# A Mamba block and a binarised feed-forward on one core: one transfer over 128 partitions for xc, z and the gated outputs, norm's affine kept off DVE, other durations in the planner

## The chip, the cores and the metric

The kernel runs on one core of one Trainium2 chip. The metric is the device time in microseconds of one execution, as a median over runs. A profiled execution, taken by the hardware profiler, stands beside it. The engines are called PE (matrix multiply), DVE (vector), ACT (scalar, activations), POOL (GpSimd) and SP (the engine that issues almost every DMA here).

## The reference, cut to what matters

The input x holds B = 8 images of C = 384 channels and L = 1024 positions, in float32. Two residual steps follow each other.

```
x = x + conv_ref(ln_c(x), ...)            # a Mamba block with an MLP
t = to_tokens(x)
x = from_tokens(t + ffn_ref(ln_t(t), ...))   # binarised weights, quantised activations

conv_ref:  t = layernorm(t) * ln_w + ln_b
           xm, z = split(t @ in_proj_w.T)              # 768 + 768 channels
           xc = silu(depthwise conv of 3 taps over positions of xm)
           dt, Bm, Cm = split(xc @ x_proj_w.T)         # 24, 16, 16
           dt = softplus(dt @ dt_proj_w.T + dt_proj_b)
           h[l] = exp(dt[l] * A) * h[l-1] + dt[l]*xc[l] * Bm[l]      # 768 x 16 states
           y = (h * Cm summed over 16) + xc * D
           t = (y * silu(z)) @ out_proj_w.T
           t = gelu(t @ mlp_w1.T + b1) @ mlp_w2.T + b2
ffn_ref:   y = t @ sign(W1 - mean).T + b1, quantised per image; gelu; the same with W2
```

The feed-forward changes images 0 to 4 only: 8 images in 5 groups of one image, and the rest stays zero.

## The kernel before

**Stages of an image.** `s1(b)` normalises the image (`norm`), applies ln_w and ln_b (`affine`, one per 128 channels), multiplies with in_proj_w, makes xc, dt and dt*xc, and z in `gate`. It works in two halves of T = 512 positions and writes xc, z, dt and dtx to DRAM. `s2(b)` is the scan. `s3(b)` reads the gated outputs yg, multiplies with out_proj_w and runs the MLP. `ffn(b)` is the second residual step. `binarise` makes the signs of W1 and W2 once, beside image 0.

**The scan.** One scan tile holds 32 channels x 4 states on 128 partitions. ACT makes `da` = exp(dt*A), POOL makes `u` = dtx*B, DVE runs the recurrence (line 888), and DVE or POOL multiplies by C (lines 905 and 902). PE adds up the states with the matrix `fold` into the PSUM tile `py` (line 838). A *unit* is one `py`: an ACT instruction puts xc*D into it, from the tile `xr`; at its end DVE multiplies by `zr`, in place, and `zr` is stored as `yg_d` (lines 855 and 861). Images 1 to 6 are scanned over the full width (`half` is None): a unit is then 64 channels x both halves, and an image has 12 units, each with two tiles per quarter of the states. Images 0 and 7 are scanned in two halves, with 128 channels x 512 positions per unit, six units per half. Image 7 keeps its gated outputs in SBUF. The rings for `xr` and `zr` have one buffer each, those for the weights `w_b` and `w_f` three.

**The layout in DRAM.** xc, z and yg are handed over as [NP, P, T]: 12 pairs of 32-channel groups, and within a pair first the 64 channels of half 0, then those of half 1. A full-width unit is one contiguous block of 128 rows of 2 KB. In `s1` and `s3`, where 128 channels of one half lie on the partitions, the same data is moved by two transfers of 64 partitions each, one for even pairs and one for odd ones (`by_pair`, line 597, and line 928). So are the units of images 0 and 7 (line 801).

**The order of the work.** Each operation is written down with an engine, an assumed duration, and the tiles it reads and writes. `Plan.run` then simulates the five engines with these durations and emits the instructions in the order in which its simulation starts them; each engine executes its own list strictly in order. `MM`, `SWITCH` (added to a group of `py` matmuls), `SIGNAL` (one engine's wait for another) and the figures of the DMA line set its clock:

```
            if e == "SP":
                dma_free = max(dma_free, end + 1.0) + op.size / 370e3
                end = dma_free + 0.9
```

Where the simulated PE would idle for over 0.7 us, it emits spare matmuls that nothing reads. `affine` is an operation of ACT by default that DVE may take (and POOL, where `pool` is set, as for the norm) when ACT is busy in the simulation. So other durations mean another order on every engine.

Of the kernel before, what the change touches and what calls it, by code (L numbers as in the profile page):

```python
# [26 lines left out]
F32 = mybir.dt.float32  # L27
# [6 lines left out]
P = 128  # L34
# [34 lines left out]


MM = 0.86
SWITCH = 0.34
BATCH = 2
SIGNAL = 0.1
IDLE = 0.7
EARLY = 2
FRONTS = 3
# [84 lines left out]
class Plan:  # L162
# [57 lines left out]
    def run(self):  # L220
# [60 lines left out]
        while left:  # L281
            best = None
            for e in self.ENGINES:
                able = [(s, op) for op in cands[e] if (s := start_of(op)) is not None]
                first = max(free[e], min(able, key=lambda a: a[0])[0]) if able else None
                if first is not None and (best is None or first < best[0]):
                    best = first, e, able, False
                for op in guests[e]:
                    s = start_of(op)
                    if s is None:  # L290
                        continue
                    s = max(free[e], s)
                    if s + HOST < free[op.engine] and (
                        first is None or s + op.others[e][0] <= first
                    ) and (best is None or s < best[0]):
                        best = s, e, [(s, op)], True
            now, e, able, guest = best
            op = able[0][1] if guest else choose(e, now, able)
            if guest:
                op.cost, op.emit = op.others[e]  # L300
            for k in op.others:
                guests[k].remove(op)
            cands[op.engine].remove(op)
            op.engine = e
            if op.settle is not None:
                op.settle(ahead("POOL", now) - ahead("DVE", now), drop)
            if op.prio[0] == 0:
                scanned = max(scanned, op.prio[1])
            left -= 1
            if e == "PE":  # L310
                while now - free[e] > IDLE and self.spare.ring.free[0:] and (
                    self.spare.ring.free[0] + SIGNAL <= free[e]
                ):

                    ring = self.spare.ring
                    heapq.heappop(ring.free)
                    self.spare.real = ring.make(self.spare.shape, self.spare.name)
                    self.fill()
                    free[e] = clock.run(free[e], MM / 2)
                    heapq.heappush(ring.free, free[e])  # L320
            for t in taken_by(op):
                heapq.heappop(t.ring.free)
                t.ring.taken[t.lane] += 1
                t.real = t.ring.make(t.shape, t.name)
            op.emit()
            cost = op.cost
            if op.table is not None and op.table != table:
                cost += LOAD_TABLE
                table = op.table
            end = free[e] = clock.run(now, cost) if e == "PE" else now + cost  # L330
            if e == "SP":
                dma_free = max(dma_free, end + 1.0) + op.size / 370e3
                end = dma_free + 0.9
            for t in op.tiles:
                if t.ring is not None:
                    t.left -= 1
                    t.last = max(t.last, end)
                    if not t.left:
                        heapq.heappush(t.ring.free, t.last)
            for n in op.next:  # L340
                n.wants -= 1
                n.ready = max(n.ready, end + n.slack + (
                    0.0 if n.engine == e != "SP" and not n.others else SIGNAL
                ))
                if not n.wants:
                    cands[n.engine].append(n)
                    for k in n.others:
                        guests[k].append(n)


class Layer:
    def __init__(self, ctx, tc, a, out):
# [38 lines left out]
        for b in range(B):  # L391
            for name in ("dt", "dtx"):
                self.dram[name, b] = handed(f"{name}_d{b}", [DI, L])

            for name in ("xc", "z", "yg"):
                self.dram[name, b] = handed(f"{name}_d{b}", [NP, P, T])
            self.dram["rows", b] = handed(f"rows_d{b}", [2 * NS, L])
            if b < NQ:
                self.dram["mid", b] = handed(f"mid_d{b}", [C, L])
                self.dram["y1", b] = handed(f"y1_d{b}", [P, KH, L])  # L400
# [6 lines left out]
        self.nc.tensor.matmul(  # L407
            first, self.ones, self.one.to_broadcast([P, T]), start=True, stop=True
        )
        self.plan.spare = self.piece("mm", [P, T], "spare")  # L410
        self.plan.fill = lambda: self.nc.tensor.matmul(
            self.plan.spare.real[:, : 2 * P], self.ones,
            self.one.to_broadcast([P, 2 * P]), start=True, stop=True,
        )

    def piece(self, ring, shape, name):
# [90 lines left out]
    def affine(self, out, in_, r, w, bias=0.0, scale=1.0, n=T, pool=False):  # L507
# [16 lines left out]

            return emit

        others = {"DVE": (c_dve(n), on(nc.vector))}
        if pool:
            others["POOL"] = (0.18 + n * 0.00095, on(nc.gpsimd))
        extra = 0.0 if plain else 0.06 if isinstance(scale, float) else 0.13  # L530
        self.plan.add("ACT", 0.16 + n * 0.00083 + extra, on_act, r=r, w=w, others=others)

    def norm(self, t, eps, scale):
# [17 lines left out]
        def spread(src, name):  # L551
            p = self.piece("mm", [P, T], name)

            def emit():
                for g in range(G):
                    one = self.ident[:, g * DQ : g * DQ + 1].to_broadcast([P, P])
                    nc.tensor.matmul(
                        p.real[:, g * TG : (g + 1) * TG], one, src.real, start=True, stop=True
                    )

            add("PE", 1.25, emit, r=[src], w=[p])
            return p

        p_sum = columns(t, "p_sum")
# [23 lines left out]
    def s1(self, b):  # L588
# [5 lines left out]

        def by_pair(name, half, t):
            d = self.dram[name, b]
            for i in range(2):
                to = d.real[i::2, half * DP : (half + 1) * DP, :].rearrange("k p l -> p k l")
                self.store(
                    to, t, lambda x, i=i: x[i * DP : (i + 1) * DP, :, :], [d[half, i]],  # L600
                    4 * DP * KD * T, 0.6,
                )

        def tiled(name, half, t):
            d = self.dram[name, b]
# [29 lines left out]
        for half, cols in enumerate(HALVES):  # L635
# [51 lines left out]
                            start=(k == 0), stop=(k == KC - 1),  # L687
                        )

            add("PE", 0.2 + KC * MM, low, r=[w, *all_m], w=[p_dbc], claim=[dbc])  # L690
            self.affine(lambda dbc=dbc: dbc.real, lambda p_dbc=p_dbc: p_dbc.real, [p_dbc], [dbc])
            p_bc = self.piece("mm", [P, TG], "p_bc")
            rows = self.piece("rstd", [P, TG], "rows")
# [61 lines left out]
    def scan(self, b, half, state):  # L755
# [30 lines left out]
        for m in range(DI // per_unit):  # L786
            py = self.piece("y", [P, T], "py")
            tiles = [range((2 * m + i) * wide, (2 * m + i + 1) * wide) for i in both]

            def rows_of(m=m):  # L790

                if half is None:
                    return [(slice(0, P), m, slice(0, P))]
                mine = slice(half * DP, (half + 1) * DP)
                return [(slice(i * DP, (i + 1) * DP), 2 * m + i, mine) for i in both]

            def unit(name):
                r = self.piece(f"{name[0]}r", [P, T], f"{name[0]}r")
                d = self.dram[name, b]
                keys = [(h, i) for h in halves for i in both]  # L800
                for at, pair, its in rows_of():
                    self.plan.add("SP", 0.35, lambda at=at, pair=pair, its=its: (
                        nc.sync.dma_start(r.real[at, :], d.real[pair, its, :])
                    ), r=[d[k] for k in keys], w=[r], size=4 * P * n // wide)
                return r

            skip = self.d_pair if half is None else self.d_unit
# [48 lines left out]
                zr.real, py.real, zr.real  # L856
            ), r=[py], w=[zr])
            d = self.dram["yg", b]
            for at, pair, its in rows_of():
                self.plan.add("SP", 0.35, lambda at=at, pair=pair, its=its, zr=zr: (  # L860
                    nc.sync.dma_start(d.real[pair, its, :], zr.real[at, :])
                ), r=[zr], w=[d[h, pair] for h in halves], size=4 * P * n // wide)

    def on_pool(self, i, q, m):

# [44 lines left out]
    def s3(self, b):  # L910
        nc, a, add = self.nc, self.a, self.plan.add
        yg_d = self.dram["yg", b]
        for half, cols in enumerate(HALVES):
# [11 lines left out]
                    late.append((w, pm))  # L925
            else:
                yg = self.piece("yg", [P, KD, T], "yg")
                for i in range(2):
                    src = yg_d.real[i::2, half * DP : (half + 1) * DP, :]
                    self.plan.add("SP", 0.6, lambda i=i, yg=yg, src=src: nc.sync.dma_start(  # L930
                        yg.real[i * DP : (i + 1) * DP, :, :], src.rearrange("k p l -> p k l")
                    ), r=[yg_d[half, m] for m in range(i, NP, 2)], w=[yg[i]],
                        size=4 * DP * KD * T)
            for m in range(KC):
                if b == B - 1:
                    w, pm = late[m]
# [1 line left out]
                else:  # L938
                    w = self.weights("w6", KD, a["out_proj_w"][m])
                    pm = self.piece("mm", [P, T], "p_out")  # L940
                    self.matmuls(pm, w, yg, 0, KD, True, True, [yg[0], yg[1]], [t2])
                self.affine(
                    lambda m=m, t2=t2: t2.real[:, m, :], lambda pm=pm: pm.real, [pm], [t2[m]]
                )
# [320 lines left out]
```

## Time and profile before

| | us |
|---|---|
| median of 3 runs | 3303.43 (3297.44 to 3304.55) |
| profiled execution | 3289.89 |
| its span, first to last instruction | 3287.1 |
| stage 0 to 345, mostly images 0 and 1 before their gated outputs | 345 |
| stage 345 to 2836, the units of images 1 to 6 | 2491 |
| stage 2836 to the end, image 7 | 451 |

In the page, "busy" is the time in which an engine had an instruction running. An engine can be busy while its instruction is held up, which a mean far above the shortest time of the same group shows. In a table by stretches the last columns are the granted PE clock, the mean busy share of the 16 DMA engines and the rate in GB/s. In the DMA issues the last figure is the median time from issue to landing. The chain of waits is followed back from the last instruction; "issue" in it is time for which the profile shows no cause.

### The profile page before, as it was taken

To read this page: it belongs to the slowest core of one execution; us is meant where nothing else is said; L and a number is where in the kernel's file an instruction comes from. 1 tells how busy PE (TensorE), PEld (TensorE's weight loads), DVE (VectorE), ACT (ScalarE), POOL (GpSimd) and SP (SyncE) were. 2 spreads that over 40 slices of the span, in tenths; PEclk is the share of its full clock that TensorE was granted. 3 is DMA by queue.
4 is the path that set the end of the run, shared out by engine and by line. 5 is a ranking of instruction groups with operands and counts; after the bars stand their busy time and mean duration, and the time that the engine had idled before them with its cause. 6 is when DMAs were issued, how large, how long until landed. Compare 5 with 4: busy or idle time off the path is not lost.

```text
span 3287.1 us, 34264 instructions
## 1 busy us (share of the span) xinstructions
PE 3136.3 (95%) x11184; PEld 1327.2 (40%) x11184; DVE 2769.7 (84%) x2139; ACT 2023.0 (62%) x2241; POOL 2848.0 (87%) x1369
## 2 busy tenths in 40 slices
PE   8988889999989999899998999999999999999999
PEld 4333434344333444334443443444433444344444
DVE  4679799899897899888898888799996998887980
ACT  4778577667655566655674665676556555565651
POOL 1688789988899989899989999989999999999970
PEclk9999999999999999999999999999999999999999
DMA  6998778857786677876688665976778666666542
GB/s 219 288 284 245 218 230 282 279 181 232 232 293 219 192 220 247 280 225 211 235 259 253 228 204 192 312 242 210 228 235 292 211 193 211 217 205 220 177 133 77
DMA packets 368083, 748.74 MB, mean 228 GB/s; under 512 B 34593, under 2 KB 111905, under 8 KB 367905
## 3 DMA queue, kind: packets, MB, share of 16 engines
q1 hardware_dynamic: 367472, 746.46, 71.4%
q8 instruction: 89, 1.46, 0.2%
q14 instruction: 90, 0.73, 0.1%
q10 hardware_dynamic: 432, 0.09, 0.0%
HBM read 566.06 MB, written 180.36 MB: 227 GB/s over the span
## 4 chain that ended last, share of the span: by engine, by line
PE 71%; DMA 8%; ACT 7%; DVE 6%; issue 3%; POOL 3%; SPq 1%; DVEq 0%; POOLq 0%; ACTq 0%
PE p_o L485 15%; PE p_y L485 14%; PE p_h L485 13%; PE py L838 8%; PE p_out L485 7%; PE p_in L485 5%; PE p_z L485 5%; DVE da L888 2%; DMA w_b<-in_mlp_w 2%; ACT da L501 2%; ACT L501 1%; POOL u L884 1%; DVE u L888 1%; DMA w_n<-bin_w 1%; PE p_dt L716 1%
## 5 line engine op out<-in xcount | busy, mean ns | idle before, releaser
L884 POOL TENSOR_TENSOR u<-dtx_r,bc 128x1024 f32<-128x1024 f32 x768 | 1790.1, 2365 | 54.0 <-DMA dtx_r<-dtx_d 32.4
L501 ACT ACTIVATE da<-dt_r,a_neg 128x1024 f32<-128x1024 f32 (+1 forms) x960 | 901.9, 945 | 549.6 <-DVE u L905 340.3
L902 POOL TENSOR_TENSOR u<-u,bc 128x1024 f32<-128x1024 f32 x352 | 829.2, 2367 | 141.0 <-DVE u L888 136.7
L888 DVE TENSOR_TENSOR_SCAN da<-da,u 128x1024 f32<-128x1024 f32 (+1 forms) x416 | 840.4, 2020 | 75.6 <-ACT da L501 40.3
L888 DVE TENSOR_TENSOR_SCAN u<-da,u 128x1024 f32<-128x1024 f32 (+1 forms) x352 | 699.0, 2009 | 84.0 <-ACT da L501 43.6
L485 PE MATMUL p_h<-t,w_b 128*128 128x512 f32 x1152 | 515.0, 601 | 17.2 <-DMA w_b<-in_mlp_w 17.2
L905 DVE TENSOR_TENSOR u<-da,bc 128x1024 f32<-128x1024 f32 x416 | 507.9, 1221 | 10.7
L485 PE MATMUL p_o<-g,w 128*128 128x512 f32 x1152 | 506.4, 595 | 0.0
L838 PE MATMUL py<-u,fold 128*32 128x512 f32 x3072 | 374.9, 602 | 5.5 <-POOL u L902 2.9
L485 PE MATMUL p_y<-gf,w_n 128*128 128x512 f32 x720 | 324.0, 605 | 22.4 <-ACT gf L501 13.4
L485 PEld LDWEIGHTS p_h<-t,w_b 128*128 128x128 f32 x1152 | 216.1, 191 | 303.5 <-issue 277.9
L485 PEld LDWEIGHTS p_o<-g,w 128*128 128x128 f32 x1152 | 216.1, 190 | 287.0 <-issue 281.5
L485 PE MATMUL p_y<-tn,w_b 128*128 128x512 f32 x720 | 324.0, 597 | 1.7 <-DVE tn L582 1.6
L501 ACT ACT_TABLE_LOAD x226 | 290.0, 1283 | 8.6 <-DVE xc L655 3.8
L485 PE MATMUL p_out<-yg,w 128*128 128x512 f32 x552 | 250.7, 606 | 14.5 <-DMA dtx_r<-dtx_d 6.0
L485 PE MATMUL p_in<-t,w_f 128*128 128x512 f32 x504 | 232.3, 608 | 16.5 <-DMA w_f<-in_in_proj_w 10.6
L485 PE MATMUL p_z<-t,w_f 128*128 128x512 f32 x504 | 226.4, 596 | 9.4 <-DMA w_f<-in_in_proj_w 5.7
L485 PEld LDWEIGHTS p_y<-gf,w_n 128*128 128x128 f32 x720 | 136.3, 193 | 208.9 <-issue 175.2
L485 PEld LDWEIGHTS p_y<-tn,w_b 128*128 128x128 f32 x720 | 133.5, 190 | 176.1 <-issue 154.7
L516 ACT ACTIVATE g<-p_h,v_vecs 128x512 f32<-128x512 f32 x156 | 105.8, 682 | 137.8 <-PE p_h L485 137.4
L838 PEld LDWEIGHTS py<-u,fold 128*32 128x32 f32 x3072 | 81.0, 110 | 265.4 <-issue 207.4
L516 ACT ACTIVATE y<-p_y,v_vecs 128x512 f32<-128x512 f32 x138 | 93.9, 682 | 129.5 <-PE p_y L485 86.7
(115 smaller groups left out, 2745.9 us busy)
## 6 DMA issues: line engine op xcount, KB each, us to landing
dtx_r<-dtx_d SPq DMA_DIRECT2D x144, 512.0 KB, 4.9
dt_r<-dt_d SPq DMA_DIRECT2D x144, 512.0 KB, 5.5
w_b<-in_mlp_w SPq DMA_DIRECT2D x192, 192.0 KB, 2.8
w<-in_mlp_w SPq DMA_DIRECT2D x96, 384.0 KB, 3.2
w_f<-in_in_proj_w SPq DMA_DIRECT2D x168, 192.0 KB, 4.2
y_d<-y SPq DMA_DIRECT2D x120, 256.0 KB, 4.2
gf<-y_d SPq DMA_DIRECT2D x20, 1536.0 KB, 9.0
xc_d<-xc SPq DMA_DIRECT2D x32, 768.0 KB, 8.8
```

What stands on the lines that cost most here:

```text
L485: self.nc.tensor.matmul(p.real, w.real[:, w0 + k, :], t.real[:, k0 + k, :], start=start and k == 0, stop=stop and k == n - 1,)
L501: lambda: self.nc.scalar.activation(out(), in_(), func, **{k: v() if callable(v) else v for k, v in kw.items()}),
L516: nc.scalar.activation(out(), in_(), AF.Identity, bias=bias, scale=scale)
L716: add("PE", MM, lambda k=k, pd=pd, dbc=dbc, w=w: nc.tensor.matmul(pd.real, w.real[:, k % KC, :], dbc.real, start=True, stop=True,), r=[dbc ...
L838: nc.tensor.matmul(py.real[p0 : p0 + DQ, :], self.fold, hc, start=False, stop=(q == NQUAD - 1), skip_group_check=True,)
L884: add("POOL", 2.36, lambda: nc.gpsimd.tensor_mul(u.real, dtx_r.real, spread(bq)), r=[dtx_r, bq], w=[u])
L888: add("DVE", (0.2 if half else 0.15) + n * 0.00209, lambda k=k, col=col: nc.vector.tensor_tensor_scan(to.real[:, k, :], da.real[:, k, :], ...
L902: add("POOL", 2.36, lambda: nc.gpsimd.tensor_mul(u.real, u.real, spread(cq)), r=[cq], w=[u])
L905: add("DVE", 1.21, lambda: nc.vector.tensor_mul(u.real, da.real, spread(cq)), r=[da, cq], w=[u])
```

## The change

Five things are edited.

1. xc, z and yg are laid out as [KD, 2, P, T]: six groups of 128 channels, then the half, then the channel within the group. `by_pair`, the yg load in `s3` and the units of images 0 and 7 become one transfer of 128 partitions each. A full-width unit takes 64 of the 128 channels of a group, from both halves.
2. `affine` with `pool` set may go to ACT or POOL, and no longer to DVE.
3. `SWITCH`, `SIGNAL`, the figures of the DMA line, the added durations in `affine`, those of `spread` in `norm` and of `low` in `s1` change, and a `DRAIN` of 0.2 us is added to every wait of another engine for PE.
4. `unread` is called up front: two POOL fills, three POOL products, two matmuls, an ACT copy and a DVE scan, with strided operands, on three buffers of the ring tag `u`; nothing reads their results.
5. The wait of out_proj for yg is on the whole tile.

```diff
-SWITCH = 0.34
+SWITCH = 0.26
-SIGNAL = 0.1
+SIGNAL = 0.05
+DRAIN = 0.2
...
-                dma_free = max(dma_free, end + 1.0) + op.size / 370e3
-                end = dma_free + 0.9
+                dma_free = max(dma_free, end + 0.8) + op.size / 395e3
+                end = dma_free + 0.75
...
-                ))
+                ) + (DRAIN if e == "PE" != n.engine else 0.0))
...
-                self.dram[name, b] = handed(f"{name}_d{b}", [NP, P, T])
+                self.dram[name, b] = handed(f"{name}_d{b}", [KD, 2, P, T])
...
+    def unread(self, sbuf, psum):
+        nc = self.nc
+        w = sbuf.tile([P, L], F32, tag="u", name="w_once", bufs=9)
+        v = sbuf.tile([P, L], F32, tag="u", name="v_once", bufs=9)
+        o = sbuf.tile([P, L], F32, tag="u", name="o_once", bufs=9)
+        pm = psum.tile([P, T], F32, tag="mm", name="p_once", bufs=3)
+        nc.gpsimd.memset(w, 0.5)
+        nc.gpsimd.memset(v, 0.5)
+        for i in (2, 4):
+            n = L // i
+            nc.gpsimd.tensor_mul(
+                o.rearrange("p (n i) -> p n i", i=i), w.rearrange("p (n i) -> p n i", i=i),
+                v[:, :n].unsqueeze(2).to_broadcast([P, n, i]),
+            )
+        nc.gpsimd.tensor_mul(
+            o.rearrange("p (n i) -> p i n", i=2), w.rearrange("p (i n) -> p i n", i=2),
+            v.rearrange("p (i n) -> p i n", i=2),
+        )
+        pairs = w.rearrange("p (n i) -> p n i", i=2)
+        for _ in range(2):
+            nc.tensor.matmul(pm[:DQ, :], self.fold, pairs[:, :, 0], start=True, stop=True)
+        nc.scalar.copy(o.rearrange("p (n i) -> p n i", i=2)[:, :, 0], w[:, :T])
+        nc.vector.tensor_tensor_scan(
+            o.rearrange("p (n i) -> p n i", i=2)[:, :, 1], v[:, :T], pairs[:, :, 1], 0.0,
+            ALU.mult, ALU.add,
+        )
...
-        others = {"DVE": (c_dve(n), on(nc.vector))}
         if pool:
-            others["POOL"] = (0.18 + n * 0.00095, on(nc.gpsimd))
+            others = {"POOL": (0.18 + n * 0.00095, on(nc.gpsimd))}
+        else:
+            others = {"DVE": (c_dve(n), on(nc.vector))}
-        extra = 0.0 if plain else 0.06 if isinstance(scale, float) else 0.13
+        extra = 0.0 if plain else 0.09 if isinstance(scale, float) else 0.18
...
-            for i in range(2):
-                to = d.real[i::2, half * DP : (half + 1) * DP, :].rearrange("k p l -> p k l")
-                self.store(
-                    to, t, lambda x, i=i: x[i * DP : (i + 1) * DP, :, :], [d[half, i]],
-                    4 * DP * KD * T, 0.6,
-                )
+            self.store(d.real[:, half].rearrange("k p l -> p k l"), t, lambda x: x, [d[half]],
+                       4 * P * KD * T)
...
-            def rows_of(m=m):
+            def rows_of(d, m=m):
                 if half is None:
-                    return [(slice(0, P), m, slice(0, P))]
-                mine = slice(half * DP, (half + 1) * DP)
-                return [(slice(i * DP, (i + 1) * DP), 2 * m + i, mine) for i in both]
+                    return d.real[m // 2, :, m % 2 * DP : (m % 2 + 1) * DP, :]
+                return d.real[m, half]
...
-                keys = [(h, i) for h in halves for i in both]
-                for at, pair, its in rows_of():
-                    self.plan.add("SP", 0.35, lambda at=at, pair=pair, its=its: (
-                        nc.sync.dma_start(r.real[at, :], d.real[pair, its, :])
-                    ), r=[d[k] for k in keys], w=[r], size=4 * P * n // wide)
+                keys = list(halves)
+                self.load(r, lambda t: t, rows_of(d), r=[d[k] for k in keys], size=4 * P * T,
+                          cost=0.35)
...
-            for at, pair, its in rows_of():
-                self.plan.add("SP", 0.35, lambda at=at, pair=pair, its=its, zr=zr: (
-                    nc.sync.dma_start(d.real[pair, its, :], zr.real[at, :])
-                ), r=[zr], w=[d[h, pair] for h in halves], size=4 * P * n // wide)
+            self.store(rows_of(d), zr, lambda t: t, [d[h, m] for h in halves], 4 * P * T, 0.35)
...
-                for i in range(2):
-                    src = yg_d.real[i::2, half * DP : (half + 1) * DP, :]
-                    self.plan.add("SP", 0.6, lambda i=i, yg=yg, src=src: nc.sync.dma_start(
-                        yg.real[i * DP : (i + 1) * DP, :, :], src.rearrange("k p l -> p k l")
-                    ), r=[yg_d[half, m] for m in range(i, NP, 2)], w=[yg[i]],
-                        size=4 * DP * KD * T)
+                self.load(yg, lambda t: t, yg_d.real[:, half].rearrange("k p l -> p k l"),
+                          r=[yg_d[half, m] for m in range(KD if b == 0 else NP)], size=4 * P * KD * T)
```

More of the change, by code (lines that the diff above doesn't have):

```diff
@@ L409, in __init__ @@
         )
+        self.unread(sbuf, psum)
         self.plan.spare = self.piece("mm", [P, T], "spare")
@@ L559, in emit @@
                     )
-            add("PE", 1.25, emit, r=[src], w=[p])
+            add("PE", 0.98, emit, r=[src], w=[p])
             return p
@@ L688, in low @@
                         )
-            add("PE", 0.2 + KC * MM, low, r=[w, *all_m], w=[p_dbc], claim=[dbc])
+            add("PE", 0.26 + KC * MM, low, r=[w, *all_m], w=[p_dbc], claim=[dbc])
             self.affine(lambda dbc=dbc: dbc.real, lambda p_dbc=p_dbc: p_dbc.real, [p_dbc], [dbc])
@@ L940, in s3 @@
                     pm = self.piece("mm", [P, T], "p_out")
-                    self.matmuls(pm, w, yg, 0, KD, True, True, [yg[0], yg[1]], [t2])
+                    self.matmuls(pm, w, yg, 0, KD, True, True, [yg], [t2])
                 self.affine(
```

## The prediction, made before the changed kernel ran

> **What bounds the kernel now.** I read the page's busy shares first, then the table by stretches, the DMA issues, the groups of line 523 with the chain of waits, and last the waits of the SP queue.
>
> ```profile
> PE 3136.3 (95%) x11184; PEld 1327.2 (40%) x11184; DVE 2769.7 (84%) x2139; ACT 2023.0 (62%) x2241; POOL 2848.0 (87%) x1369
> ...
> q1 hardware_dynamic: 367472, 746.46, 71.4%
> ```
>
> PE has work for 95% of the span, 100.3 us of it being the planner's spare matmuls. POOL and DVE follow closely. The 16 DMA engines are on average busy 71.4%: less than a third of their time is free.
>
> ```profile
> 345.00:2836.00 2491.00, 2394.93 (x8634) 1003.90 (x8633) 2212.40 (x1598) 1550.69 (x1607) 2292.18 (x1054) 0.99 0.74 234
> 82.00:400.00 318.00, 274.09 (x1025) 121.14 (x1024) 248.47 (x243) 227.06 (x309) 251.43 (x156) 0.94 0.86 264
> 1340.00:1350.00 10.00, 6.28 (x20) 3.25 (x20) 7.61 (x8) 7.35 (x9) 7.21 (x4) 1.00 1.05 405
> ```
>
> Columns after the length: busy PE, weight load, DVE, ACT, POOL, clock, DMA share, GB/s. The first row is the stage in which images 1 to 6 are scanned: 72 units of 34.6 us, DMA share 0.74 at 234 GB/s. The second is the busiest long stretch (0.86). The third is the fastest of all 10 us stretches: 405 GB/s, or 25.3 GB/s per engine. Over the whole run an engine moves 746.46 MB / (0.714 x 16 x 3287.1 us) = 19.9 GB/s while it is busy.
>
> ```profile
> xr<-xc_d SPq DMA_DIRECT2D x72, 256.0 KB, 3.0
> zr<-z_d SPq DMA_DIRECT2D x72, 256.0 KB, 3.2
> yg_d<-zr SPq DMA_DIRECT2D x72, 256.0 KB, 2.2
> yg<-yg_d SPq DMA_DIRECT2D x28, 768.0 KB, 10.4
> dt_d<-dt SPq DMA_DIRECT2D x16, 1536.0 KB, 7.5
> ```
>
> Each unit of that stage loads xr and zr and stores yg_d, once each, and they land in 2.2 to 3.2 us. A yg load of half the partitions takes longer (10.4 us) than a store of twice the bytes over 128 (7.5 us).
>
> ```profile
> L523 DVE TENSOR_SCALAR t<-t,v_vecs 128x512 f32<-128x512 f32 x12 | 29.4, 2468 | 0.1
> ```
>
> The chain of waits at that line:
>
> ```profile
> 932.40 0.26 DVE t L523
> 932.66 9.73 issue
> 942.39 0.02 DVEq L888
> 942.41 4.75 issue
> 947.17 0.54 DVE t L523
> ```
>
> Twelve instructions with a shortest time of 0.519 us average 2.468 us. Two in a row took 15.38 us from 932.32, while POOL ran without a gap, and the chain carries 9.73 + 4.75 = 14.5 us of that. Three more took 8.39 us from 2350.86 (3.4 us in the chain).
>
> ```profile
> SPq L803 <- DMA yg_d<-zr: 51.1, 41, 6.7
> ```
>
> SP issues in order, and the next zr load already waits behind the landing of the yg_d store.
>
> [...]
>
> **The change part by part**, against the profiled execution of 3289.89 us, which lies 13.5 us under the median of 3303.43; differences are added to the median.
>
> The unit transfers. With the layout [KD, 2, P, T] a unit of a full-width scan takes `d.real[m // 2, :, m % 2 * DP : ..., :]`: two blocks of 64 rows, far apart. The instruction lists show the DRAM side as 2 x 64 x 512 where it was 128 x 512, in 72 xr loads, 72 zr loads and 72 yg_d stores. [...] In 345 to 2836 us the kernel moves 234 x 2491 = 583 MB, of it 216 x 0.262 = 56.6 MB in these transfers. Engines 0 and 1 would each carry (583 - 56.6)/16 + 56.6/2 = 32.9 + 28.3 = 61.2 MB, where now it is 36.4. At 25.3 GB/s that is 2419 us of work, at 19.9 GB/s 3075 us, in a stage of 2491 us. I take the fast rate, as the 14 other engines are then lightly loaded, and the fill of the busiest long stretch, 0.86: 2419/0.86 = 2813 us, **+322 us**. Bounds: filled completely at the fast rate it fits (0 from bandwidth alone); 0.86 at the slow rate gives +1085. Queued behind them are all weights, dt_r and dtx_r of SP: PE takes a w_b of 192 KB every 2.58 us (12 records of p_h, two such weights, are 5.15 us in the chain) from three buffers, a cover of 3 x 2.58 - 2.8 (its landing) = 4.9 us, less than one such transfer (131,072 / 25.3 GB/s = 5.2 us). Each DMA in the list also waits for that eight before it, so SP cannot run ahead of a backlog.
>
> The merged half transfers (xc_d, z_d stores, yg loads, unit transfers of image 0). SP issues 106 instructions fewer. yg should land in 7.5 to 9.0 us (dt_d, gf of that size) instead of 10.4; the chain has it twice: -3 us, between -6 and 0, since other loads may be late next.
>
> The affine off DVE. The lists give ACT 8 more (at 0.80 us, under its 62%), POOL 4 more (at 0.83 us, +3.3 us at most). DVE loses 29.4 us; the chain carried 14.5 + 3.4 = 18. PE has other work in part of it: -10 us, between -23 (all above 12 x 0.519) and 0.
>
> The planner. Spare matmuls go from 200 to 170 (30 x 0.50 = 15 us of PE, but they fill waits: 0); ACT table loads from 228 to 221, hidden under ACT. The order differs almost everywhere, which no row prices: 0, between -15 and +15.
>
> The unread operations. POOL: two fills of 1024 (0.95 us each, estimated from 0.205 for 128 columns and 0.10 for one) and three products (2.365 each, the row of line 884[...]). They end near 10.2 us; behind them waits an ACT copy (0.59), and behind that the first `mean`, at 8.02 us before. PE has two matmuls that wait for `fold` (7.2 us), and four spares behind them, ahead of the first p_sum (7.09). So +3.5 us; between +1 (p_sums waited 1.96 us for a DMA at 17.27 anyway) and +7.
>
> Sum without the unit transfers: -3 - 10 + 3.5 = -9.5, from -43 to +25. With them: 3303.4 - 9.5 + 322 = **3616**.
>
> **The rivals.**
>
> A, on the other side: the three unit transfers still spread over 16 engines[...]. Price -9.5 us, giving 3294 (3260 to 3328). For it: no transfer here ever had such a shape, so nothing measured speaks against. It wins if xr still lands in under 4 us; from 5 us on it loses.
>
> B: two engines, but they keep up, and only latency is paid. Landings grow by (131,072 - 16,384)/25.3 GB/s = 4.5 us. A load of zr has most of a 34.6 us unit to come, so it hides; SP stands 72 x 4.5 = 324 us longer behind the yg_d store, and after the weights' 4.9 us of cover about 1 us per unit reaches PE: +72, giving 3366 (3300 to 3440). For it: 2419 us fits into 2491. Against: that needs two queues that never run empty.
>
> C: the new order of the plan is worse than the old; with 16 engines at most +25, or 3328.
>
> **How the numbers follow.** Two engines that bind: 0.60, its own range 3440 to 3900. B: 0.20. A and C, all engines used: 0.20, of it 0.12 faster, 0.04 within, 0.04 slower by 0.2% (6.6 us; the three runs lie 7.1 us apart). B and the main case together leave 0.01 for each of faster and same. The range takes most of A, and the fill of 0.86 at 23.4 GB/s as its upper end: 3268 to 3850.
>
> **What would show it.** Landing medians of xr, zr and yg_d of 7 us or more (right) or about 3 us (A). In right order: weights land late, at 6 us or more for w_b where it is 2.8; "DMA w_b" and "DMA w" rise in the waits of PE; the DMA share, a mean over 16, falls below 0.70 although PE waits for DMA; SP's wait for yg_d<-zr rises from 51 to over 300 us; stages of image 0 and from 2836 us on keep their length. In every case no DVE instruction of t<-t,v_vecs remains, and the first `mean` comes near 11 us. The prediction is wrong if the stage of 72 units stays near 2491 us.

## The result, and the profile after

| | before | after |
|---|---|---|
| median, us | 3301.43 (4 runs) | 4029.66 (4 runs, 4026.44 to 4038.27) |
| profiled execution, us | 3289.89 | 4038.27 |
| its span, us | 3287.1 | 4036.5 |
| granted PE clock, mean | 0.985 | 0.907 |

The ratio is 1.2211, with an interval of 1.2186 to 1.2235. The changed kernel is slower by 728 us. The forecast was slower by 313 us (3616, range 3268 to 3850): the direction held, and so did the cause, two DMA engines that carry a share meant for 16 (shown below); the time lies above the range.

From the page of the kernel after, the busy shares, the main DMA queue and the shares of the chain of waits:

```profile
PE 3299.8 (82%) x11128; PEld 1380.6 (34%) x11128; DVE 2753.3 (68%) x2132; ACT 2015.0 (50%) x2239; POOL 2859.7 (71%) x1378
...
q1 hardware_dynamic: 362752, 746.44, 55.8%
...
PE 48%; DMA 31%; DVE 6%; POOL 5%; ACT 4%; issue 3%; SPq 2%; ACTq 0%; DVEq 0%; POOLq 0%
```

The same 746 MB are moved, and the mean share of the 16 DMA engines falls from 71.4% to 55.8%. Yet waiting for DMA now makes up 31% of the chain, where it was 8%:

```profile
PE 71%; DMA 8%; ACT 7%; DVE 6%; issue 3%; POOL 3%; SPq 1%; DVEq 0%; POOLq 0%; ACTq 0%
```

PE falls from 95% to 82%. So the DMA engines are emptier on average and the others wait for them.

The table by stretches (length, then busy PE, weight load, DVE, ACT, POOL, clock, DMA share, GB/s), cut at 345 us and at 3557 us, where the last yg_d store of images 1 to 6 is issued:

```profile
0.00:345.00 345.00, 302.57 (x1229) 138.69 (x1230) 238.71 (x249) 232.06 (x314) 221.85 (x153) 0.96 0.78 262
345.00:3557.00 3212.00, 2533.51 (x8559) 1050.01 (x8558) 2196.48 (x1595) 1546.34 (x1601) 2303.16 (x1058) 0.89 0.55 182
3557.00:4036.00 479.00, 463.76 (x1342) 191.94 (x1341) 318.16 (x290) 236.57 (x325) 334.72 (x168) 0.98 0.48 154
```

Of the 749 us by which the two spans differ, 721 lie in the stage of the 72 units (3212 instead of 2491) and 28 behind it (479 instead of 451). The stage runs at 182 GB/s, not 234. The trace also has the start and the length of every DMA packet. Counted from those of 512 bytes and more, exactly two packets are in flight for 26% of the stage, where before it was 1.4%.

Who waits, from the waits of the engines (total us, times, longest):

```profile
POOL u L904 <- DMA dtx_r<-dtx_d: 383.8, 49, 15.8
PE p_h L514 <- DMA w_b<-in_mlp_w: 149.0, 31, 15.5
PE p_y L514 <- DMA w_n<-bin_w: 86.0, 12, 13.9
```

Before, the first two were:

```profile
POOL u L884 <- DMA dtx_r<-dtx_d: 32.4, 9, 6.6
PE p_h L485 <- DMA w_b<-in_mlp_w: 17.2, 9, 4.0
```

Both wait for transfers of 192 and 512 KB whose own shape did not change. The waits of the SP queue:

```profile
SPq L493 <- DMA yg_d<-zr: 317.8, 77, 10.6
```

It was 51.1. A piece of the chain shows how the two combine (start, length, what):

```profile
1512.87 14.86 DMA xr<-xc_d
...
1528.26 13.00 DMA y_d<-y
...
1548.35 8.31 DMA yg_d<-zr
...
1558.28 18.65 DMA yg<-yg_d
...
1577.07 7.89 PE p_out L514 x12
```

Four transfers, 55 us in sum, stand one behind the other in the chain before PE gets its yg. In the kernel before, xr landed in 3.0 us and a yg half in 10.4 (medians). For the changed kernel the page has no times to landing, so the signs that I had named for landing are read from the chain and from the experiments.

### The profile page after: what moved, and what is told of

It is laid out like the page before. It is cut to its first block, busy times and chain, and to the rows that moved or that the text cites. A ratio compares the mean times of both kernels' runs of the same rounds, so it can differ in the third digit from the quotient of the medians.

```text
span 4036.5 us, 34023 instructions
## 1 busy us (share of the span) xinstructions
PE 3299.8 (82%) x11128; PEld 1380.6 (34%) x11128; DVE 2753.3 (68%) x2132; ACT 2015.0 (50%) x2239; POOL 2859.7 (71%) x1378
## 3 DMA queue, kind: packets, MB, share of 16 engines
q1 hardware_dynamic: 362752, 746.44, 55.8%
## 4 chain that ended last, share of the span: by engine, by line
PE 48%; DMA 31%; DVE 6%; POOL 5%; ACT 4%; issue 3%; SPq 2%; ACTq 0%; DVEq 0%; POOLq 0%
PE p_o L514 10%; PE p_h L514 9%; PE p_y L514 9%; PE p_out L514 5%; DMA w_b<-in_mlp_w 5%; PE py L861 5%; DMA y_d<-y 4%; DMA yg_d<-zr 4%; PE p_z L514 4%; DMA w_n<-bin_w 3%; PE p_in L514 3%; POOL u L904 3%; DMA w<-in_mlp_w 2%; DMA w_f<-in_in_proj_w 2%; DMA yg<-yg_d 2%
## 5 line engine op out<-in xcount | busy, mean ns | idle before, releaser
L514 PE MATMUL p_h<-t,w_b 128*128 128x512 f32 x1152 | 555.3, 637 | 149.3 <-DMA w_b<-in_mlp_w 149.0
L514 PE MATMUL p_o<-g,w 128*128 128x512 f32 x1152 | 530.9, 618 | 88.8 <-DMA w<-in_mlp_w 71.0
L514 PE MATMUL p_y<-gf,w_n 128*128 128x512 f32 x720 | 344.0, 636 | 101.2 <-DMA w_n<-bin_w 86.0
L514 PEld LDWEIGHTS p_h<-t,w_b 128*128 128x128 f32 x1152 | 227.4, 203 | 464.0 <-issue 412.5
L514 PE MATMUL p_y<-tn,w_b 128*128 128x512 f32 x720 | 351.7, 636 | 42.1 <-ACT y L545 35.6
L514 PEld LDWEIGHTS p_o<-g,w 128*128 128x128 f32 x1152 | 225.4, 199 | 393.1 <-issue 301.7
L514 PE MATMUL p_out<-yg,w 128*128 128x512 f32 x552 | 264.8, 635 | 91.6 <-DMA w<-in_out_proj_w 54.0
L514 PE MATMUL p_z<-t,w_f 128*128 128x512 f32 x504 | 239.4, 626 | 44.6 <-DMA w_f<-in_in_proj_w 40.4
L514 PEld LDWEIGHTS p_y<-gf,w_n 128*128 128x128 f32 x720 | 144.8, 205 | 299.8 <-issue 221.0
L514 PEld LDWEIGHTS p_out<-yg,w 128*128 128x128 f32 x552 | 109.9, 204 | 237.2 <-issue 178.7
```

The source lines that it names most:

```text
L514: self.nc.tensor.matmul(p.real, w.real[:, w0 + k, :], t.real[:, k0 + k, :], start=start and k == 0, stop=stop and k == n - 1,)
```

## The experiments

Every ratio is against the kernel before on the same chip. Where a difference of ratios is given in us, it is taken times 3295 us.

### Two transfers of 64 rows instead of one of 2 x 64

`e1_split` is the changed kernel with each full-width unit transfer issued as two, inside the same planned operation (for full-width units alone), so that the order of the plan stays as it is:

```diff
-                self.load(r, lambda t: t, rows_of(d), r=[d[k] for k in keys], size=4 * P * T,
-                          cost=0.35)
...
+                    src = rows_of(d)
+                    for h in both:
+                        nc.sync.dma_start(r.real[h * DP : (h + 1) * DP, :], src[h])
...
-            self.store(rows_of(d), zr, lambda t: t, [d[h, m] for h in halves], 4 * P * T, 0.35)
...
+                    for h in both:
+                        nc.sync.dma_start(dst[h], zr.real[h * DP : (h + 1) * DP, :])
```

> The changed kernel with one edit: each of the 216 full-width unit transfers goes out as two of 64 rows, one per half, in place of one of 2 x 64 rows. The planned order of everything else is unchanged. Theory[...]: about 3294 us, the prediction's sum without the unit transfers, between 3260 and 3328; DMA share back near 0.71; SP's wait for yg_d<-zr near 50 us. Rival 1 (the new order of the plan or the merged transfers cost the time): stays within 100 us of 4030.

Measured: 3314.47 us, ratio 1.0049 (1.003 to 1.0067). From its page and its table by stretches:

```profile
q1 hardware_dynamic: 369232, 746.47, 68.4%
...
w_b<-in_mlp_w SPq DMA_DIRECT2D x192, 192.0 KB, 2.8
```

```profile
345.00:2840.00 2495.00, 2370.94 (x8554) 994.57 (x8547) 2186.77 (x1592) 1542.69 (x1595) 2298.60 (x1055) 0.98 0.71 233
```

SP issues 216 instructions more, and 712 us (1.2211 less 1.0049) are gone. The stage is back at 2495 us and the weight lands in 2.8 us. All but 16 us of the slowdown hang on the shape of these 216 transfers.

### The layout alone

`e2_layout_alone` is the kernel before with only the new layout: the half-wide transfers stay two of 64 partitions, and plan and order are those of before.

```diff
-                self.dram[name, b] = handed(f"{name}_d{b}", [NP, P, T])
+                self.dram[name, b] = handed(f"{name}_d{b}", [KD, 2, P, T])
...
-                    return [(slice(0, P), m, slice(0, P))]
+                    return [(slice(0, P), (m // 2, slice(0, 2), slice(m % 2 * DP, (m % 2 + 1) * DP)))]
```

> The kernel before with one edit: xc, z and yg are laid out as [KD, 2, P, T], so that a full-width unit is 2 x 64 rows; half transfers stay two of 64 partitions, and plan, affine and start are those of before. Theory of two engines: the whole loss, 3950 to 4150 us. Rival 1 (order of the plan, merged transfers): within 30 us of 3303. Half of the loss would say that plan and layout work together.

Measured: 4046.73 us, ratio 1.2273 (1.2248 to 1.2297). The layout is sufficient for the loss as well as necessary.

### The transfers by themselves

`m1_transfers` leaves the whole computation out and moves data only: chains of 12 transfers of 256 KB with one buffer, streams, groups of one such transfer and five of 512 KB, and round trips through DRAM. It is one execution.

```diff
+    rows = lambda i: x[i % B, :P, :T]
+    pair = lambda i: x[i % 7 : i % 7 + 2, :64, :T]
```

> Only transfers, none of the reference's computation; the output is zeros. 256 KB loads one after the other, as 128 rows and as 2 x 64 rows; then back to back; then each kind mixed with five loads of 512 KB; then round trips through DRAM. Two engines: 2 x 64 rows take 5.2 us of data each (131,072 B at 25.3 GB/s) and land about 4.5 us later than 128 rows (7 to 8 us against 3); back to back one per 5.2 us at 51 GB/s; in the mix a group (262 KB on 2 x 64 rows and 2.6 MB on 16 engines) takes (131 + 164) KB / 25.3 GB/s = 11.7 us if the fast rate holds beside other traffic, and 14.8 us if it is 19.9 GB/s. If all 16 engines are used: no difference between the two shapes, about 7 to 9 us per group.

The SP queue in its timeline (start, length):

```profile
0.73 30.41 SPq L30 DMA_DIRECT2D one_rows<-in_x  x12
31.18 84.22 SPq L30 DMA_DIRECT2D one_pair<-in_x  x12
```

The table by stretches (clock, DMA share and GB/s are the last three): the stream of pairs, the groups with one pair, the same groups with 128 rows in its place.

```profile
150.00:300.00 150.00, 0.00 (x0) 0.00 (x0) 1.00 0.13 51
327.00:603.00 276.00, 0.00 (x0) 0.00 (x0) 1.00 0.69 222
641.00:790.00 149.00, 0.00 (x0) 0.00 (x0) 1.00 1.03 408
```

A transfer of 2 x 64 rows takes 84.22/12 = 7.02 us where 128 rows take 2.53: 4.5 us more, the figure of the prediction. A stream of them has a share of 0.13, which is two engines of 16 (0.13 x 16 = 2.1), at 51/2 = 25.5 GB/s each. That it is always the same two follows from the stream, which stays at 51 GB/s; which two is not seen, and the numbers 0 and 1 in the prediction and in the expectations are not measured. In the mixed groups, with the five transfers of 512 KB taken as spread evenly over 16 engines (the groups of rows alone have a share of 1.03), two engines carry 131,072 + 5 x 32,768 = 294,912 bytes per group. 21 groups took 603.29 - 327.43 us, 13.14 each: **22.4 GB/s** per engine, not 25.5, and between the 11.7 and 14.8 us that were set out. If the last packets in flight are theirs, the two engines hardly stood idle there: two or more packets are in flight for 99.9% of these groups, and exactly two for 28%. The groups of rows alone take 7.08 us.

### How the loss grows with the number of transfers

Three kernels leave only some of the unit transfers on two engines and split the others as e1 does: `d72_xr_on_two` the xr loads, `d72_store_on_two` the yg_d stores, `d144_loads_on_two` both loads. The edit of the first, beside the split of the store:

```diff
+                    if half is None and name == "z":
```

> The changed kernel with the yg_d stores and zr loads split; only the 72 xr loads stay 2 x 64. Theory: as d72_store_on_two, 3315 to 3370 us. Rival, same cost for each: 3552. If only SP's wait for the store counted: 3314, as e1_split.

> The changed kernel with the 144 xr and zr loads split; only the 72 yg_d stores stay 2 x 64. Theory: 35.3 + 9.4 = 44.7 MB, 2320 us at 22.4 GB/s and 0.86, under the 2491 us of the stage: no loss from the rate, at most some latency, 3315 to 3370 us. Rival, same cost for each: 3552. Rival, SP blocked behind the landing of the store is the main cost: above 3550, and far above d72_xr_on_two.

> The changed kernel with the 72 yg_d stores split into two of 64 rows; the 144 xr and zr loads stay 2 x 64. Theory: engines 0 and 1 bind by what they carry. In the stage they carry (582.9 - 37.7)/16 + 18.9 = 52.9 MB; at 22.4 GB/s (the rate of the mixed groups in m1_transfers) and a fill of 0.86 that is 2750 us instead of 3177: about 3570 us in all. Rival (every such transfer costs the same, 715/216 = 3.3 us, by its latency): 3314 + 144 x 3.3 = 3790 us.

The stage in the table by stretches, up to the issue of the last yg_d store, in this order:

```profile
345.00:2986.00 2641.00, 2410.04 (x8560) 1004.80 (x8559) 2188.60 (x1592) 1540.61 (x1595) 2298.89 (x1056) 0.97 0.67 221
```

```profile
345.00:3021.00 2676.00, 2423.09 (x8556) 1007.31 (x8557) 2191.37 (x1593) 1546.27 (x1599) 2304.76 (x1059) 0.96 0.65 218
```

```profile
345.00:3273.00 2928.00, 2488.10 (x8559) 1032.17 (x8558) 2192.62 (x1592) 1544.87 (x1599) 2304.41 (x1059) 0.92 0.61 199
```

The load on the two engines is an estimate, worked out as in the prediction, from each row's bytes; the rate is that load over the stage.

| kernel | on two engines | us | ratio | load, MB | stage, us | GB/s |
|---|---|---|---|---|---|---|
| e1 | 0 | 3314.47 | 1.0049 (1.003 to 1.0067) | 36.3 | 2495 | 14.6 |
| xr | 72 | 3459.79 | 1.0517 (1.0486 to 1.0547) | 44.7 | 2641 | 16.9 |
| store | 72 | 3498.17 | 1.0633 (1.06 to 1.0667) | 44.7 | 2676 | 16.7 |
| xr, zr | 144 | 3736.8 | 1.1359 (1.1305 to 1.1413) | 52.9 | 2928 | 18.1 |
| after | 216 | 4029.66 | 1.2211 (1.2186 to 1.2235) | 61.3 | 3212 | 19.1 |

The first 72 cost 2.1 (xr: 0.0468 x 3295 / 72) to 2.7 us each, the next 3.9 and the last 3.9. There is no flat part: 72 transfers leave the two engines at 44.7 MB, which 22.4 GB/s moves in 1996 us, and still 154 to 192 us are lost. So filling up by bytes is not the whole cause. Neither main side of the expectations was met: bytes, rate and fill gave 3315 to 3370 us at 72 and 3570 at 144, too little each time, and an equal cost for each transfer gave 3552 and 3790, too much each time. The waits of the SP queue and of PE, first xr, then store:

```profile
SPq L830 <- DMA yg_d<-zr: 49.5, 52, 3.6
```

```profile
SPq L830 <- DMA yg_d<-zr: 349.1, 71, 7.6
```

```profile
PE p_h L514 <- DMA w_b<-in_mlp_w: 49.1, 20, 6.0
```

```profile
PE p_h L514 <- DMA w_b<-in_mlp_w: 54.8, 24, 7.0
```

In e1 the last of these was:

```profile
PE p_h L514 <- DMA w_b<-in_mlp_w: 6.3, 6, 2.3
```

SP stands 300 us longer behind yg_d in the store kernel, and that kernel is only 38 us slower. This wait is thus mostly hidden. What both kernels have in common is the weight that comes late. That bytes of a slow transfer stood ahead of it on the two engines would fit, but was not shown.

The traces of these five kernels hold the same 11128 matmul records, so PE's time can be compared part by part (us; the waits are the sums over all waits of PE for that engine):

| kernel | span | PE busy | PE waits for DMA | PE waits for ACT | clock |
|---|---|---|---|---|---|
| e1 | 3311 | 3131 | 78 | 48 | 0.982 |
| xr | 3457 | 3173 | 167 | 58 | 0.969 |
| store | 3494 | 3185 | 190 | 56 | 0.967 |
| xr, zr | 3741 | 3248 | 329 | 91 | 0.937 |
| after | 4037 | 3300 | 524 | 144 | 0.907 |

At 72 transfers PE waits 89 to 112 us more for DMA than in e1, and the same matmuls keep it busy 42 to 54 us longer. At 216 it is 446 and 169 us.

### A planner that knows the price

`p2_planner_told` is the changed kernel, with eight times the bytes given to the planner for the 216 transfers; what is moved is the same.

```diff
-            self.store(rows_of(d), zr, lambda t: t, [d[h, m] for h in halves], 4 * P * T, 0.35)
+            self.store(rows_of(d), zr, lambda t: t, [d[h, m] for h in halves],
+                       (8 if half is None else 1) * 4 * P * T, 0.35)
...
```

> The changed kernel; the planner is given eight times the bytes for the 216 transfers of 2 x 64 rows (5.3 us of its DMA line each), so it places the instructions behind them later. The chip's work is the same. Theory: the two engines bind by what they carry, and the order can fill them only a little better: 3850 to 4030 us. Rival (the loss comes from an order made for landings of 3 us, with SP standing before loads that could go): under 3650 us.

Measured: 3730.65 us, ratio 1.134 (1.1288 to 1.1393). Its table by stretches:

```profile
345.00:2967.00 2622.00, 2474.81 (x9343) 1162.07 (x9332) 2156.44 (x1529) 1469.46 (x1526) 2276.70 (x1048) 0.98 0.62 208
2967.00:3723.00 756.00, 736.40 (x2186) 332.93 (x2184) 346.27 (x342) 293.08 (x382) 356.68 (x178) 0.99 0.46 149
```

Of the loss, 287 us (1.2211 less 1.134) come back with another order, more than the theory allowed (3850 to 4030) and less than the rival asked for (under 3650). The new order brings 1982 records of spare matmuls where there were 340, and a clock of 0.98 in the stage; what each of these is worth was not separated. Worked out in the same way, the two engines carry 58.9 MB in 2622 us, 22.5 GB/s over the stage. Two or more packets are in flight for 96% of it, against 86% in the changed kernel. Both engines cannot have been at work for longer than that, so by this estimate each moved at least 23.4 GB/s while at work here, and 22.1 in the changed kernel. What the order moved out of the stage is paid behind it, 756 us instead of 479.

### The other edits

All of these have the unit transfers split or are the kernel before, so that the small terms can be seen. `e3_split_no_unread` is e1 without `unread`:

```diff
-        self.unread(sbuf, psum)
```

> As e1_split, and the unread operations up front are left out. Prediction's term for them: 3.5 us less than e1_split (1 to 7). If the late start is absorbed by later waits: no difference beyond 2 us.

Measured: 3312.8 us, ratio 1.0049 (1.0031 to 1.0066), that of e1. The unread operations cost nothing that can be measured.

`e4_split_affine_dve` is e3 with the affine allowed on DVE as well:

```diff
-            others = {"POOL": (0.18 + n * 0.00095, on(nc.gpsimd))}
+            others = {"DVE": (c_dve(n), on(nc.vector)),
+                      "POOL": (0.18 + n * 0.00095, on(nc.gpsimd))}
```

> As e3_split_no_unread, but norm's affine may go to DVE again (11 of them do). Prediction's term: 10 us slower than e3_split_no_unread (0 to 23), about 3323; stalled DVE instructions of t<-t,v_vecs come back. Rival (taking the affine off DVE brought nothing or costs): equal to e3_split_no_unread within 5 us, or faster.

Measured: 3310.45 us, ratio 1.0051 (1.0037 to 1.0065). The group is back with its stalls, and the time is e3's:

```profile
L551 DVE TENSOR_SCALAR t<-t,v_vecs 128x512 f32<-128x512 f32 x11 | 22.1, 2044 | 0.1
```

`e5_split_old_durations` is e3 with the planner's durations of before:

```diff
-SWITCH = 0.26
-SIGNAL = 0.05
-DRAIN = 0.2
+SWITCH = 0.34
+SIGNAL = 0.1
+DRAIN = 0.0
...
-                dma_free = max(dma_free, end + 0.8) + op.size / 395e3
-                end = dma_free + 0.75
+                dma_free = max(dma_free, end + 1.0) + op.size / 370e3
+                end = dma_free + 0.9
...
```

> As e3_split_no_unread, with the durations of the kernel before in the planner (no DRAIN, old DMA line). If the new order of the plan is what made the rest of the change 16 us slower where 9.5 us less were forecast: about 3296 or less (-13 from merges and affine would give 3283). If it is not: 3313.

Measured: 3287.93 us, ratio 0.9972 (0.9962 to 0.9982). The new durations cost 1.0049 - 0.9972, 25 us, and without them the rest is faster than the kernel before.

`e6_affine_alone` is the kernel before with the affine kept off DVE:

```diff
-        others = {"DVE": (c_dve(n), on(nc.vector))}
         if pool:
-            others["POOL"] = (0.18 + n * 0.00095, on(nc.gpsimd))
+            others = {"POOL": (0.18 + n * 0.00095, on(nc.gpsimd))}
+        else:
+            others = {"DVE": (c_dve(n), on(nc.vector))}
```

> The kernel before with one edit: norm's affine may not go to DVE. Prediction's term: 10 us faster than before (0 to 23). Rival: the order of the plan changes with it and swallows it, within 10 us of before on either side.

Measured: 3305.25 us, ratio 1.003 (1.0018 to 1.0042), 10 us slower. DVE has no affine left, but p_out waits 12.7 us for yg where it waited 5.2.

`e7_merge_alone` is e5 with the affine on DVE again, so of the whole change only the new layout with the merged half-wide transfers is left (the unit transfers go out as two of 64 rows, and the wait of out_proj is on the whole tile):

```diff
-            others = {"POOL": (0.18 + n * 0.00095, on(nc.gpsimd))}
+            others = {"DVE": (c_dve(n), on(nc.vector)),
+                      "POOL": (0.18 + n * 0.00095, on(nc.gpsimd))}
```

> e5 with the affine allowed on DVE again: of the whole change only the layout with merged transfers for the half-wide blocks is left (unit transfers two of 64 rows, durations of before, nothing unread). Theory 1, the parts add up: the affine kept off DVE cost 10 us in e6 (ratio 1.003) and the merged transfers bring the rest of e5's 0.9972, so this kernel gives 0.9972 - 0.003 = 0.994, about 3277 us, with DVE t<-t,v_vecs back at 12 instructions. Rival, the parts do not add up, because each edit makes another order on every engine: the kernel lies within 0.3% of the kernel before (0.997 to 1.003) whatever e5 and e6 gave apart. The prediction's price for the merged transfers, -3 us, would be 0.999.

Measured: 3284.61 us, ratio **0.9957** (0.9944 to 0.9971), the lowest ratio of all, though its interval meets that of e5. Of its groups, the affine on DVE:

```profile
L551 DVE TENSOR_SCALAR t<-t,v_vecs 128x512 f32<-128x512 f32 x8 | 10.7, 1362 | 0.1
```

Theory 1 (0.994) lies just under the interval and the rival (from 0.997) at its upper end, so neither is decided for; the prediction's 0.999 is excluded. The DMA issues of this kernel give for the merged yg:

```profile
yg<-yg_d SPq DMA_DIRECT2D x14, 1536.0 KB, 8.5
```

## Why the prediction was right in kind and wrong in size

**The unit transfers: two engines, right; their rate, wrong.** That a transfer of 2 x 64 rows goes to two engines was a supposition when the prediction was made; m1 shows it, with the share of 0.13. All that was to be seen if two engines bind is there: weights late (149.0 us of waits for w_b), the DMA share at 0.558, SP's wait at 317.8 us (51 + 324 was said). Image 0 reaches its first yg load 10 us later (357.6 instead of 347.2), and the end is 28 us longer, where both were to keep their length. The step that failed is "I take the fast rate, as the 14 other engines are then lightly loaded". The fast rate, 25.3 GB/s, is what two engines do alone (25.5). Beside transfers over all 16 they did 22.4 in the groups of m1. With that rate the same sum gives 61.2 MB / (22.4 x 0.86) = 3177 us, +686 us where +322 was predicted and 712 measured. A rate 13% too high halved the term, because a stage of 2491 us is subtracted from it.

That the other factor fits is in part luck. 19.1/22.4 = 0.85 is near the fill of 0.86, but that fill came from a stretch in which an engine moved 264 / (16 x 0.86) = 19.2 GB/s while busy, so it was joined to a rate that it had not been seen with. Nor is it a constant: the same working gives 2320 us at 72 transfers, where 2641 and 2676 were measured, and 2750 at 144, where it was 2928, and in p2 the order alone brought two or more packets into flight for 96% of the stage. So the sum is right at 216 and not in general.

**A term that was missing: the clock.** The prediction put nothing down for slower matmuls. PE needed 169 us more than in e1 for the same number of them, at a clock of 0.907 instead of 0.982. Whether the stage would have been shorter at the full clock, or PE would only have waited longer, is not shown.

**The range.** The term had a bound of +1085 us of its own, from the busy rate of 19.9 GB/s, and the range was then cut at 23.4 GB/s, a value that no row gave. The 22.4 of m1 lies between the two.

**Rival B.** That two engines can keep up and only latency is paid is half right. Its SP wait was well sized and is mostly hidden, as it said. Its +72 us for 216 transfers was far too little: the first 72 alone cost 154 to 192. The formula of bytes, rate and fill gives nothing at 72 transfers, so a loss of the kind that B describes, weights that come late (49.1 and 54.8 us of waits for w_b, against 6.3 in e1), is there well before the two engines are full by their bytes. I had put the two as alternatives, and the runs show no point at which one gives way to the other. At 72 most of the loss of the profiled executions (146 and 183 us) is PE's waits for DMA (89 and 112), the rest mainly slower matmuls; what each late transfer brings to it was not separated.

**Rival A** fell with m1, e1 and e2. **The merged half transfers**: -3 us predicted, between -6 and 0; e7 has -14 (-10 to -18). Right in sign, mis-sized, and outside of its bounds; e7 has an order of its own and split unit transfers too, so the 8.5 us of yg against 10.4 is not shown to be all of it.

**The affine off DVE**: -10 us predicted. It cost 10 us alone (e6), nothing under the new durations (e3 against e4) and about 5 under the old (e5 against e7, whose intervals overlap). The stall at that line is real (2468 ns a piece, the shortest 519; what held them up was not shown) and did leave, but its 18 us in the chain of one execution were not the kernel's to gain: another order comes with its removal, and in e6 PE waits longer for yg. Why ACT and POOL taking it costs anything was not settled.

**The planner**: 0 predicted, within 15; e3 less e5 is +25 us. Rival C had a worse order cost up to 25 us for the whole change with all 16 engines; that sum is +16 (e1), within C's bound, and it is the small part of the loss. Which of the durations does it was not tried.

**The unread operations**: +3.5 predicted, 0 measured. The first `mean` came later than said, at 14.43 us (timeline of the kernel after: start, length, what, idle time before and its releaser), and it did not matter:

```profile
7.64 3.62 PE L438 MATMUL p_once<-w_once,fold 128*32 128x512 f32 x4 [4.65 <-DVE fold L461]
...
14.43 0.28 ACT L545 ACTIVATE mean<-p_sum 128x128 f32<-128x128 f32 x1 [3.97 <-PE p_sum L572]
```

The first p_in starts at 31.87 us with them, and at 31.48 without (e3), with p_sums waiting for a DMA of w ahead of it in both.

**The sum of the rest**: -9.5 predicted, +16 measured (e1), made of -14 (merge), +5 (affine), +25 (durations) and 0 (unread) along the kernels e7, e5, e3 and e1. The parts add up because each is the step from one of these to the next. Taken in another order they differ: the affine alone is +10 (e6), and beside the slow transfers the rest is a gain of 20 us (1.2211 against 1.2273 for the layout alone).

## What to carry to other kernels

Before two transfers are merged into one, look at the shape that the DRAM side gets: 256 KB as 2 x 64 rows went to two engines here (a share of 0.13 in m1), and the 216 such transfers, issued as two of 64 rows each, cost 712 us less, a fifth of the time of the kernel before. Where a stage is bound by a few engines, take their rate from a mix like the kernel's own, take rate and fill from the same stretch, and carry the whole uncertainty into the range, since the stage's old length is subtracted from it. A stall that the chain of waits shows in one execution need not come back as time: here 18 us in the chain left and nothing was gained. Where a planner orders the work, each edit must be measured in its own order.

## What the runs showed of the hardware

- In m1 a stream of 2 x 64 rows has a share of 0.13, two DMA engines of 16, and they move 25.5 GB/s each. Beside transfers that by themselves have a share of 1.03 it is 22.4, by the estimate above, with two or more packets in flight for 99.9% of the time. Why the rate falls was not tried.
- A mean DMA share hides this bound: the changed kernel shows 0.55 in its stage, lower than before, with exactly two packets in flight for 26% of it.
- PE's matmuls took longer in the kernels in which it waited more. The same matmul p_h, after and in e1 (busy, mean ns, then idle before):

```profile
L514 PE MATMUL p_h<-t,w_b 128*128 128x512 f32 x1152 | 555.3, 637 | 149.3 <-DMA w_b<-in_mlp_w 149.0
```

```profile
L514 PE MATMUL p_h<-t,w_b 128*128 128x512 f32 x1152 | 512.4, 598 | 9.4 <-DMA w_b<-in_mlp_w 6.3
```

In the stage PE is busy 2534 us against 2371, at a clock of 0.89 against 0.98. The kernel after shows a piece of this from 1563 us on: PE waits 13.41 us for yg, the granted clock is 0.50 from 1570 to 1582 us, and 12 matmuls of p_out take 7.89 us; from 1582 us on the clock is 0.99 to 1.00, and the next 12 take 5.32. The five kernels above agree: the mean clock falls from 0.982 to 0.907 as PE's waits for DMA rise from 78 to 524 us.

- Of the unread products of POOL, the two with a repeated operand took 2.00 and 2.12 us, and the one that writes every second element 2.35, no more than the products of the kernel's own scan (2.36).
